# Four steps of a segment-attention loop in another order

## The chip, the cores and the metric

The program runs on one core of a Trainium2 chip. The metric is the device time of one execution in microseconds (us); for the kernel before it is 2229.49 us, the median of three runs (2226.88 to 2230.01).

A core has engines that each work through a queue of their own: TensorE (PE, matrix products, with the weight loads shown apart as PEld), VectorE (DVE), ScalarE (ACT), GpSimd (POOL) and SyncE (SP, which here only issues DMAs). They wait for each other through semaphores. PE writes its results to PSUM, which is divided into banks; the other engines read them there.

## The reference

The network is a decoder of four layers on x of 16 x 256 x 128 floats; each layer has an attention, a cross-attention and a feed-forward part, each followed by a residual and a layer norm. The change lies in one of these twelve parts, the attention of layer L1. Sixteen heads of 8 channels; the 256 positions of a batch form four segments of 64. Each segment attends to itself with all its 64 keys, and to the segments one and two away with every fourth of their keys (SEG is 64, DIL 4, NN 2):

```
def _attn(q, k, v):
    scores = jnp.einsum('bshqd,bshkd->bshqk', q, k) / math.sqrt(q.shape[-1])
    a = jax.nn.softmax(scores, axis=-1)
    return jnp.einsum('bshqk,bshkd->bshqd', a, v)
...
out = _attn(q, k, v)
dil_idx = jnp.arange(0, SEG, DIL)
kd = k[:, :, :, dil_idx, :]
vd = v[:, :, :, dil_idx, :]
seg_ids = jnp.arange(S)
w = 1.0 / (2 * NN)
for off in range(1, NN + 1):
    for sign in (-1, 1):
        n = seg_ids + sign * off
        valid = (n >= 0) & (n < S)
        nc = jnp.clip(n, 0, S - 1)
        cross = _attn(q, kd[:, nc], vd[:, nc])
        out = out + jnp.where(valid[None, :, None, None, None], cross * w, 0.0)
...
return out @ Wo + bo
```

## The kernel before

The whole network is one program; its parts follow one another, with x kept in SBUF in two forms: `xt` (128 positions by 128 channels, 32 tiles) and `xT` (channels by 4096 positions). The part of the change is `layer_a1`. It treats the 16 batches one after another, two batches being a group of 512 positions (8 groups), in a loop over rounds b that is a software pipeline. Products and their users are:

- `project`: one product 128x512 gives q or k of a group in the PSUM bank `m`; ACT adds the bias and writes it to SBUF.
- `keys`: POOL multiplies k of a batch with a mask of heads, once for the own segments (`kb4`) and once for every fourth key (`kbd`). Then a product with 32 rows can treat one head.
- `own_scores` and `far_scores`: scores in two PSUM tiles named `sc`, which ACT turns into exponentials, `eo` and `ed` (the latter is called `e` in the profile).
- `values`: five pairs of small products into `m`; DVE adds the bias and spreads them into `vxs`.
- `sums`: denominators into the bank `den` (products at L340), then numerators of the own segments into `num`; DVE takes the reciprocals (L949) and weights them (L950).
- `scaled`: products that spread the reciprocals over the rows of `ed`, again into the two `sc` tiles, after which DVE multiplies `ed` in place (L969, two instructions); one more product spreads them for the own part, ACT copies it (L971), DVE multiplies (L972).
- `far_sums`: numerators of the far segments; DVE adds both parts to `oTn` (L981).
- `out`: the output product of a group into `m`, then `tail`: DVE adds the residual (L458) and takes statistics (L393, L394), POOL the reciprocal root (L381 to L399). The last step of the norm, on ACT (L404), is put off until `settle` in the next round. `transposed` later turns the finished group back into `xT`: four PE transposes into `m` and a copy on ACT (L355).

Two things set the order. `in_order` ties each PE instruction to the one before it, so that PE works in exactly the order in which the code calls it. On the other engines a planner orders the instructions: GpSimd and VectorE run some of them earlier than the code's order has them (the first two `xb` of L435 stand ahead of the first `keys`, an `oTn` among the statistics of an `out`). The line in force for PSUM is:

```
    with s.banks(sc=(2, 2), den=(1, 1), num=(2, 1), m=(1, 1)), s.in_order(), s.deferring():
```

So there are two `sc` tiles for three users a round (own scores, far scores, the spread reciprocals), and a single bank `m` for `project`, `values`, `transposed` and `out`. All products are issued through the helpers at L336, L340 and L343, so that the profile shows these lines and the tile names tell the steps apart. The DMAs of the part load weights for later parts; no step of the loop issues one.

Of the kernel before, what the change touches and what calls it, by code (L numbers as in the profile page):

```python
# [19 lines left out]
B, S, D, SC = 16, 256, 128, 64  # L20
NT = B * S
NTI = NT // 128
NG = NT // 512
# [629 lines left out]
def evac(s, out, ps, bias=None):  # L653

    if bias is None:
        s.nc.scalar.copy(out, ps)
    else:
        s.nc.scalar.activation(out, ps, AF.Identity, bias=bias)
# [207 lines left out]
def layer_a1(s, w):  # L866
# [16 lines left out]
    q, k, kb, eo, ed, oT, num, rw = {}, {}, {}, {}, {}, {}, {}, {}  # L883

    def project(d, n, g, wt, bias):
        ps = s.bank("m")
        s.mm(ps, wt, s.xT[:, 512 * g:512 * g + 512])
        d[g] = s.work(n, [128, 512])
        evac(s, d[g], ps, bias)

    def keys(b):
        kb[b] = [s.work(n, [128, m, 4, 64]) for n, m in (("kb4", 4), ("kbd", 1))]
        kk = k[b // 2][:, S * (b % 2):S * (b % 2) + S]
        nc.gpsimd.tensor_tensor(kb[b][0], kk.rearrange("p (g k) -> p g k", g=4).unsqueeze(2).broadcast_to([128, 4, 4, 64]),
                                hm4.unsqueeze(1).broadcast_to([128, 4, 4, 64]), ALU.mult)
        nc.gpsimd.tensor_tensor(kb[b][1][:, 0], kk[:, 0:S:4].unsqueeze(1).broadcast_to([128, 4, 64]), hm4, ALU.mult)

    def values(b):
        xb = s.xT[:, S * b:S * b + S]
        ps = s.bank("m")  # L900
        for g in range(5):
            xs = xb[:, 64 * g:64 * g + 64] if g < 4 else xb[:, 0:S:4]
            for a in range(2):
                s.mm(ps[64 * a:64 * a + 64, 64 * g:64 * g + 64], xs, wv[:, :, a, :])
        v = ps[:, 0:320].rearrange("p (g i u d) -> p g i u d", g=5, i=4, u=2)
        dst = vxs[b % 2].rearrange("p g i (u x) -> p g i u x", u=2)
        for a in range(2):
            h = slice(64 * a, 64 * a + 64)
            for u in range(2):
                nc.vector.tensor_tensor(dst[h, :, :, u, 8 * a:8 * a + 8], v[h, :, :, u, :],  # L910
                                        bv[h, :, u, a, :].unsqueeze(1).broadcast_to([64, 5, 4, 8]), ALU.add)

    def own_scores(b):
        qb = q[b // 2][:, S * (b % 2):S * (b % 2) + S]
        sc = [s.bank("sc", [128, 2, 4, 2, 64]) for _ in range(2)]
        for g in range(4):
            for u in range(2):
                for i in range(4):
                    r = slice(32 * i, 32 * i + 32)
                    s.mm(sc[i // 2][:, i % 2, g, u, :], kb[b][0][r, g, 2 * u:2 * u + 2, :].rearrange("p j k -> p (j k)"),  # L920
                         qb[r, 64 * g:64 * g + 64])
        eo[b] = s.work("eo", [128, 4, 4, 2, 64])
        for h in range(2):
            s.latest = nc.scalar.activation(eo[b][:, 2 * h:2 * h + 2], sc[h], AF.Exp, scale=8 ** -0.5)

    def far_scores(b):
        qb = q[b // 2][:, S * (b % 2):S * (b % 2) + S]
        sc = [s.bank("sc", [128, 2, 2, S]) for _ in range(2)]
        for u in range(2):
            for i in range(4):  # L930
                r = slice(32 * i, 32 * i + 32)
                s.mm(sc[i // 2][:, i % 2, u, :], kb[b][1][r, 0, 2 * u:2 * u + 2, :].rearrange("p j k -> p (j k)"), qb[r, :])
        ed[b] = s.work("e", [128, 4, 2, S])
        for h in range(2):
            s.latest = nc.scalar.activation(ed[b][:, 2 * h:2 * h + 2], sc[h], AF.Exp, scale=8 ** -0.5)

    def sums(b):

        den = s.bank("den", [128, 2, S])
        for u in range(2):  # L940
            for i in range(4):
                s.part(den[32 * i:32 * i + 32, 0, :], sd[:, u, :], ed[b][:, i, u, :], u == 0, False)
        for g in range(4):
            for u in range(2):
                for i in range(4):
                    s.part(den[32 * i:32 * i + 32, 0, 64 * g:64 * g + 64], so[:, u, :], eo[b][:, i, g, u, :],
                           False, u == 1)
        rc = s.work("rcT", [128, S])
        nc.vector.reciprocal(rc, den[:, 0, :])  # L949
        nc.vector.tensor_tensor(rc, rc, w["wq"], ALU.mult)  # L950
        rw[b] = den, rc
        num[b] = s.bank("num", [128, 2, S])
        for g in range(4):
            for u in range(2):
                for i in range(4):
                    s.mm(num[b][32 * i:32 * i + 32, 0, 64 * g:64 * g + 64], vxs[b % 2][:, g, i, 32 * u:32 * u + 32],
                         eo[b][:, i, g, u, :], u == 0, u == 1)

    def scaled(b):
        den, rc = rw[b]  # L960
        sc = [s.bank("sc", [128, 2, 2, S]) for _ in range(2)]
        for u in range(2):
            for i in range(4):
                r = slice(32 * i, 32 * i + 32)
                s.mm(sc[i // 2][:, i % 2, u, :], rd[r, u, :], rc[r, :])
        s.mm(den[:, 1, :], w["ro"], rc)
        for h in range(2):
            e = ed[b][:, 2 * h:2 * h + 2]
            nc.vector.tensor_tensor(e, e, sc[h], ALU.mult)  # L969
        ro = s.work("ro", [128, S])  # L970
        nc.scalar.copy(ro, den[:, 1, :])  # L971
        nc.vector.tensor_tensor(ro, ro, num[b][:, 0, :], ALU.mult)  # L972
        rw[b] = ro

    def far_sums(b):
        for u in range(2):
            for i in range(4):
                s.mm(num[b][32 * i:32 * i + 32, 1, :], vxs[b % 2][:, 4, i, 32 * u:32 * u + 32], ed[b][:, i, u, :],
                     u == 0, u == 1)
        oT[b] = s.work("oTn", [128, S], bufs=3)  # L980
        nc.vector.tensor_tensor(oT[b], rw[b], num[b][:, 1, :], ALU.add)  # L981

    def out(g):
        y = s.bank("m", [128, 4, D])
        for j in range(4):
            s.mm(y[:, j, :], oT[2 * g + j // 2][:, 128 * (j % 2):128 * (j % 2) + 128], w["o"])
        s.tail(g, y, s.biased(g, w["r_bo"]), transpose=False, act=True)

    with s.banks(sc=(2, 2), den=(1, 1), num=(2, 1), m=(1, 1)), s.in_order(), s.deferring():
        project(q, "qT", 0, w["q"], w["bq"])  # L990
        project(k, "kTs", 0, w["k"], w["bk"])
        keys(0)
        keys(1)
        values(0)
        project(q, "qT", 1, w["q"], w["bq"])
        own_scores(0)
        far_scores(0)
        for b in range(B + 4):
            if b + 1 < B:
                own_scores(b + 1)  # L1000
            if 1 <= b <= B:
                far_sums(b - 1)
            if b < B:
                sums(b)
            if b + 1 < B:
                far_scores(b + 1)
                values(b + 1)
            s.settle()
            g = (b + 3) // 2
            if g < NG:  # L1010
                project(*((k, "kTs", g, w["k"], w["bk"]) if b % 2 == 0 else (q, "qT", g, w["q"], w["bq"])))
            if b < B:
                scaled(b)
            if b % 2 == 1 and 3 <= b and b // 2 - 2 >= 0 and b // 2 - 2 < NG:
                s.transposed(b // 2 - 2)
            if b % 2 == 1 and 3 <= b <= B + 1:
                out(b // 2 - 1)
            if b + 2 < B:
                keys(b + 2)


def layer_x1(s, w, gate):
# [943 lines left out]
def normalized(s, nd):  # L1966
# [7 lines left out]

LAYERS = (("a0 x0", layer_x0), ("f0", layer_f0),
          ("a1", layer_a1), ("x1", layer_x1), ("f1", layer_f1),
          ("a2", layer_a2), ("x2", layer_x2),
          ("f2 a3", layer_a3), ("x3 f3", layer_last))
# [29 lines left out]
```

## Time and profile before

The profile shows one execution of 2229.6 us, of which the span from the first to the last instruction is 2227.8 us.

| What | Value | How to read it |
|---|---|---|
| PE busy | 1795.3 us, 81% of the span | average over all parts |
| DVE, ACT, POOL busy | 1133.0, 857.9, 811.0 us | 51%, 39%, 36% |
| `layer_a1`, from its first own scores in round 0 to the last transposes | 296.9 to 542.3 us | about a ninth of the span |
| PE busy from 296.9 to 516.3 | 183.95 of 219.40 us | granted clock 0.92 on average there |
| PE busy from 516.3 to 542.3 | 14.60 of 26.00 us | the end of the part, granted clock 0.76 |
| DVE, ACT, POOL busy from 296.9 to 516.3 | 106.95, 84.94, 53.56 us | none is near its limit |

The granted clock is the share of full speed at which PE was allowed to run; in this trace it is 1.0 or 0.5 at any moment, and changes in steps of 3.41 us.

### The profile page before, as it was taken

The numbers are of one execution on the slowest core, as the hardware profiler recorded it, in microseconds if no ns is written. First come the engines' busy times: TensorE is split into PE (matmuls) and PEld (weight loads), VectorE is DVE, ScalarE is ACT, GpSimd is POOL, SyncE is SP. The second block draws the span as 40 slices with busy tenths as digits, with TensorE's granted clock in tenths as the row PEclk, the third lists the DMA queues.
The fourth block names the chain that finished last, engine by engine and source line by source line (L and its number), as shares of the span: only waits on it lengthen the run. The fifth ranks groups of instructions, "written<-read, shape, count | busy, mean of one in ns | idle before, by whom it ended". The sixth has DMA issues, their size and how long they took to land.

```text
span 2227.8 us, 39433 instructions
## 1 busy us (share of the span) xinstructions
PE 1795.3 (81%) x16572; PEld 1132.3 (51%) x16572; DVE 1133.0 (51%) x2808; ACT 857.9 (39%) x1267; POOL 811.0 (36%) x956
## 2 busy tenths in 40 slices
PE   6784388886999836949784789987789988999998
PEld 3451256664777624625452556654445544555554
DVE  5677624544366663145476677746725552322231
ACT  6565633432333201322354222225646653223221
POOL 2432322222244325755434334444536652111110
PEclk8896569997999956969896899988979998999999
DMA  3000000001011221430000000010000000000000
GB/s 114 4 3 21 1 2 3 3 3 45 1 30 29 71 51 45 76 88 0 6 14 20 1 1 1 2 41 23 2 1 2 2 1 1 5 5 5 5 10 10
DMA packets 45649, 41.59 MB, mean 19 GB/s; under 512 B 6880, under 2 KB 42144, under 8 KB 44832
## 3 DMA queue, kind: packets, MB, share of 16 engines
q1 hardware_dynamic: 35456, 31.22, 4.5%
q0 software_dynamic: 5632, 4.33, 1.5%
q10 hardware_dynamic: 4384, 3.52, 0.5%
q8 instruction: 130, 2.13, 0.4%
q14 instruction: 47, 0.39, 0.1%
HBM read 28.44 MB, written 10.62 MB: 18 GB/s over the span
## 4 chain that ended last, share of the span: by engine, by line
PE 56%; DVE 18%; POOL 11%; issue 7%; ACT 5%; DMA 2%; POOLq 0%; DVEq 0%; SPq 0%; ACTq 0%
PE p L336 14%; PE m L336 12%; PE sc L336 11%; PE y L336 6%; PE nd L336 3%; POOL rs L383 2%; PE nd L340 2%; PE den L340 2%; DVE rcT L1969 2%; PE m L343 2%; POOL acc L1318 2%; PE num L336 2%; DVE st L393 1%; ACT xt L404 1%; DVE r L458 1%
## 5 line engine op out<-in xcount | busy, mean ns | idle before, releaser
L336 PE MATMUL p<-h,w_f 128*128 128x512 f32 x512 | 222.3, 592 | 0.4 <-DVE h L1820 0.4
L336 PE MATMUL sc<-qT,kb 32*128 32x256 f32 (+1 forms) x2816 | 184.3, 381 | 42.6 <-DVE qT L650 17.2
L381 POOL TENSOR_SCALAR ve<-mv 128x4 f32<-128x4 f32 x128 | 30.6, 239 | 427.1 <-DVE mv L394 423.7
L336 PEld LDWEIGHTS sc<-qT,kb 32*128 32x128 f32 x2816 | 129.6, 204 | 94.3 <-issue 61.2
L343 PE MATMUL m<-ident,xt 128*128 128x128 f32 x448 | 87.8, 318 | 104.0 <-ACT xt L404 47.4
L336 PEld LDWEIGHTS p<-h,w_f 128*128 128x128 f32 x512 | 96.7, 190 | 119.8 <-issue 117.9
L1905 ACT ACTIVATE e<-sc 128x1024 f32<-128x1024 f32 x128 | 124.0, 1021 | 74.2 <-PE sc L336 73.4
L383 POOL TENSOR_TENSOR rs<-ve,nhalf 128x4 f32<-128x4 f32 x128 | 134.3, 1049 | 6.3
L343 PEld LDWEIGHTS m<-ident,xt 128*128 128x128 f32 x448 | 59.1, 156 | 132.9 <-ACT xt L404 54.8
L393 DVE BATCH_NORM_STATS2 st<-r 128x6 f32<-128x128 f32 x480 | 119.6, 272 | 3.3
L435 POOL TENSOR_TENSOR xb<-xt,r_x 128x512 f32<-128x512 f32 x48 | 60.8, 1271 | 152.2 <-DVE r L1763 76.9
L1969 DVE RECIPROCAL rcT<-nd 128x256 f32<-128x256 f32 x48 | 84.1, 1751 | 62.3 <-PE nd L336 62.3
L355 ACT COPY xT<-m 128x512 f32<-128x512 f32 x104 | 60.0, 581 | 139.2 <-PE m L343 138.5
L404 ACT ACTIVATE xt<-r,nm,rs 128x128 f32<-128x128 f32 x176 | 72.5, 484 | 95.0 <-POOL nm L399 95.0
L1825 ACT ACTIVATE h<-p,w_f 128x512 f32<-128x512 f32 x64 | 44.0, 687 | 153.6 <-PE p L336 153.5
L336 PE MATMUL m<-xT,w_a 128*128 128x512 f32 x144 | 82.0, 685 | 25.7 <-DVE vxs L910 18.9
L407 DVE TENSOR_SCALAR xt<-r,mv,rs 128x128 f32<-128x128 f32 x208 | 66.8, 382 | 59.6 <-POOL rs L383 59.6
L1831 DVE TENSOR_TENSOR ys<-y,r_f 128x512 f32<-128x512 f32 x8 | 5.5, 691 | 175.4 <-PE y L336 175.4
L578 ACT ACTIVATE e<-sc 128x1024 f32<-128x1024 f32 x64 | 61.9, 1019 | 62.6 <-PE sc L336 62.6
L1626 DVE TENSOR_TENSOR a<-sc,cst 128x1024 f32<-128x1024 f32 x64 | 75.0, 1208 | 14.4 <-PE sc L336 14.3
L394 DVE BATCH_NORM_AGGREGATE mv<-st 128x2 f32<-128x6 f32 x512 | 80.7, 167 | 0.1
L1094 ACT ACTIVATE e<-sc 128x1024 f32<-128x1024 f32 x32 | 32.8, 1024 | 110.0 <-PE sc L336 110.0
(423 smaller groups left out, 4075.2 us busy)
## 6 DMA issues: line engine op xcount, KB each, us to landing
acc<-xt SPq DMA_DIRECT2D x16, 256.0 KB, 2.8
mw<-in_moe SPq DMA_DIRECT2D x8, 512.0 KB, 4.1
yx<-acc SPq DMA_DIRECT2D x12, 256.0 KB, 3.6
w_f<-in_w_f SPq DMA_DIRECT2D x1, 2824.0 KB, 10.5
w_x<-in_w_x SPq DMA_DIRECT2D x1, 2336.5 KB, 9.8
xt<-in_x SPq DMA_DIRECT2D x8, 256.0 KB, 7.5
rows<-xn SPq DMA_DIRECT2D x8, 256.0 KB, 2.5
out_x<-xt SPq DMA_DIRECT2D x8, 256.0 KB, 2.3
```

The costliest lines, as they stand in the source:

```text
L336: self.put(self.nc.tensor.matmul(out=out, lhsT=lhsT, rhs=rhs, start=start, stop=stop))
L340: self.put(self.nc.tensor.matmul(out=out, lhsT=lhsT, rhs=rhs, start=start, stop=stop, skip_group_check=True))
L343: self.put(self.nc.tensor.transpose(out, in_, self.ident if ident is None else ident))
L383: nc.gpsimd.tensor_tensor(rs, ve, self.nhalf[:, :n], ALU.pow)
L393: nc.vector.bn_stats(st[:, j, :], r[:, j, :])
L394: nc.vector.bn_aggr(mv[:, j, :], st[:, j, :])
L404: ins, front = nc.scalar.activation(out[:, j, :], r[:, j, :], AF.Identity, bias=nm[:, j:j + 1], scale=rs[:, j:j + 1]), self.latest
L407: ins, front = nc.vector.tensor_scalar(out[:, j, :], r[:, j, :], mv[:, j, 0:1], rs[:, j:j + 1], ALU.subtract, ALU.mult), self.mark
L578: s.latest = nc.scalar.activation(eu, sc[h], AF.Exp, scale=8 ** -0.5)
L1626: s.mark = nc.vector.tensor_tensor(a[:, h, :, :], sc[h].rearrange("p i j k -> p (i j) k"), tri, ALU.mult)
L1905: nc.scalar.activation(e[:, 2 * h:2 * h + 2, :, :], sc[h], AF.Exp, scale=8 ** -0.5)
L1969: s.nc.vector.reciprocal(rc, nd[:, 1, :])
```

## The change

The same instructions are issued, in another order. In a round, the projection moves from behind `values` to ahead of `sums`; the masking of keys moves from the round's end to right behind `sums`; `transposed` moves from odd rounds to the next even round, for which the loop gets one round more. `values` keeps its place behind `far_scores`.

```diff
-        for b in range(B + 4):
+        for b in range(B + 5):
             if b + 1 < B:
                 own_scores(b + 1)
             if 1 <= b <= B:
                 far_sums(b - 1)
+            g = (b + 3) // 2
+            if g < NG:
+                project(*((k, "kTs", g, w["k"], w["bk"]) if b % 2 == 0 else (q, "qT", g, w["q"], w["bq"])))
             if b < B:
                 sums(b)
+            if b + 2 < B:
+                keys(b + 2)
             if b + 1 < B:
                 far_scores(b + 1)
                 values(b + 1)
             s.settle()
-            g = (b + 3) // 2
-            if g < NG:
-                project(*((k, "kTs", g, w["k"], w["bk"]) if b % 2 == 0 else (q, "qT", g, w["q"], w["bq"])))
             if b < B:
                 scaled(b)
-            if b % 2 == 1 and 3 <= b and b // 2 - 2 >= 0 and b // 2 - 2 < NG:
-                s.transposed(b // 2 - 2)
+            if b % 2 == 0 and 0 <= b // 2 - 3 < NG:
+                s.transposed(b // 2 - 3)
             if b % 2 == 1 and 3 <= b <= B + 1:
                 out(b // 2 - 1)
-            if b + 2 < B:
-                keys(b + 2)
```

## The prediction

> **What bounds the stretch.** I read the page first (PE 81% busy, no other engine over 51%), then the chain of waits through the rounds, then the timeline at the end of the loop. The chain has each link's start, length and work:
>
> ```profile
> 362.29 2.00 PE sc L336 x60
> 364.29 1.00 PE num L336 x16
> 365.29 1.76 PE den L340 x80
> 367.04 0.89 PE num L336 x64
> 367.94 1.08 PE sc L336 x16
> 369.01 0.87 PE m L336 x20
> ...
> 371.18 1.10 PE m L336 x2
> 372.28 1.09 PE sc L336 x16
> ...
> 373.39 2.36 DVE e L969 x2
> ...
> 386.88 0.63 PE den L336 x2
> 387.51 0.45 PE m L343 x4
> 387.96 0.02 issue
> 387.98 0.59 ACT xT L355
> 388.58 0.04 issue
> 388.62 1.16 PE m L336 x8
> 389.78 1.94 PE sc L336 x64
> ```
>
> This is round 4, from its own scores at 362.29 through far sums, denominators, numerators, far scores, values, projection and `scaled` to the two DVE multiplications; round 5 starts its own scores at 375.80. So a round is a ring of **13.51 us** in which PE stands still twice: 1.30 us between values (ended 369.88) and projection (371.18), because both use the one bank `m`, which DVE must empty first; and at the end, while DVE multiplies and the `sc` tiles are not free. The last five lines are an odd round with transposes: there the ring doesn't end with DVE but with bank `m` again, transposes, ACT copy, output product.
>
> **Projection ahead of the sums.** In its new place bank `m` was last used by transposes or the output product of the round before. Their readers, the ACT copy (0.59) and the DVE addition (0.69, behind 2.36 of multiplications and 0.41 of L972), are done about 1.1 us after the own scores begin; the projection comes 3.0 us after that. So it doesn't wait, and costs its 1.10 us. Its reader on ACT (0.68) stands behind the own exponentials, which end about 4 us into the round, and is done near 4.8; values want `m` at 7.9. No wait there either.
>
> What is late next, once `scaled` no longer stands behind the projection? Its products need the two `sc` tiles, and those are read by the exponentials of the far scores. Rounds 13 and 14 show it already, since no projection is left for them. Timeline of round 13:
>
> ```profile
> 497.73 1.94 ACT L935 ACTIVATE e<-sc 128x1024 f32<-128x1024 f32 x2 [5.24 <-PE sc L336]
> ...
> 499.72 1.13 PE L336 MATMUL sc<-rcT,w_a 32*128 32x256 f32 x12 [0.21 <-ACT e L935]
> 500.50 2.35 DVE L969 TENSOR_TENSOR e<-e,sc 128x1024 f32<-128x1024 f32 x2 [0.78 <-PE sc L336]
> ```
>
> From the start of the exponentials to that of the multiplications it is 500.50 - 497.73 = 2.77 us (round 14: 513.55 - 510.77 = 2.78). In round 4 it is 373.39 - 369.05 = 4.34. The new round is 2.00 + 1.00 + 1.10 + 1.76 + 0.89 + 1.08 + 0.02 + 2.77 + 2.36 + 0.04 = **13.02 us**, so 0.49 is won, not the 2.4 us of stall and product that leave the old place. The reciprocals are not later: they end 1.76 + 0.42 after the denominators, `scaled` comes 0.89 + 1.08 + 1 after them. Projections exist in rounds 0 to 12: 13 x 0.49 = **6.4 us**. Bounds: 0 if something holds the projection up for half a microsecond, 13 x 1.57 = 20 if it found a gap on PE; there is none in front of the sums, so the lower working stands.
>
> **Keys behind the sums.** Profile of waits: PE waits 7.9 us, in 7 rounds, for POOL's `kb`. But only the first four products of the own scores wait for it (346.52 in round 2, after `kb` of 1.89 us); the other sixty start 0.04 us after the DVE multiplications end (347.16). I cost the removal at 0. The new place gives POOL the masks some 8 us earlier: four instructions, 1.89 + 0.72 twice, 5.2 us in an even round. Queued behind them could be the norm of a group (about 1.8 us on POOL), whose result ACT takes only behind the far exponentials, some 5 us later; that cover suffices. No DMA moves, SP's queue holds nothing of this loop.
>
> **Transposes in even rounds.** In odd rounds 5 to 13 the time from the multiplications' start (386.90) to the end of the own scores (391.72) is 4.82; without transposes the output product starts right behind `den`, 0.63 + 1.16 fit into the 2.36, and it is 2.36 + 0.04 + 2.00 = 4.40. Won: 5 x 0.42 = **2.1 us**. In even rounds 0.63 + 0.45 lie within the 2.36 too: cost 0; without that cover 0.45 each, 8 times.
>
> **The end.** Before, the order in rounds 16 and 17 is transposes of group 6, then the output product of group 7. The chain shows the price:
>
> ```profile
> 531.19 1.65 ACT xt L404 x4
> ...
> 533.40 0.59 ACT xT L355
> ...
> 534.04 2.09 PE m L336 x8
> ```
>
> The output product at 534.04 waits for the norm of group 6, only because of its place. Its own input (`oTn`, L981) is ready at 529.15. After the change group 6 is turned in round 18, and group 5, finished long before, in round 16. The output product can run at 529.2 and, at the full clock that holds until 532.7, end at 530.35 instead of 536.13; the chain behind it (addition, statistics, POOL, norm, last transposes) keeps its 6.2 us. Won: **5.8 us**. The other bound is 0.6: in the code the norm of group 6 (settle of round 16) stands ahead of the ACT copy of group 5's transposes. If ACT keeps that order, bank `m` is free only at 532.85 + 0.59, and the output product starts at 533.5. I take 5.8, since the planner puts `oTn` among the statistics as soon as it is ready, and this is the same case.
>
> **The clock.** A round with half clock is dear: round 1 (own scores 313.61 to 330.39) takes 16.78 us with 6.83 us of half clock, against 13.51, so 0.48 per microsecond. Here a rule speaks against the change, since it takes the projection out of the sparse part of the round. The Trainium skill (page "TensorE: Matmul & The Clock Gate", section "Why this matters for your kernels") says that gaps over some 3 us between bursts bring the half clock back. No gap inside a full round is over 1.6 us, so by the rule neither order loses clock. The windows of 3.41 us (busy: PE, PEld, DVE, ACT, POOL; then the clock) say otherwise:
>
> ```profile
> 344.98:348.39 3.41, 2.03 (x50) 1.53 (x50) 2.46 (x3) 0.37 (x1) 3.41 (x3) 1.00 0.00 0
> 348.39:351.81 3.42, 3.42 (x45) 2.16 (x44) 0.12 (x1) 1.94 (x2) 1.28 (x2) 0.50 0.02 5
> ```
>
> PE was busy for 2.03 of 3.41 us, and the clock halved. A window with 2.09 (355.22) didn't bring it down. When I count each product's columns by the share of the array that it fills (32 of 128 rows: a quarter), the windows (taken 0.2 us earlier) before a half clock have under some 1550 columns, the others more. In the new rounds, the worst window is the end of an even round plus the own scores (1024 columns): under the limit when a window starts within some 0.7 us, one time in five. Rounds 0 to 4, with neither transposes nor, mostly, output products, stay as they were. From 296.9 to 516.3 I count 34 us of half clock before, and about as much after; term 0. Ends: if the early rounds keep their clock, 12 us less, -6; if pairs of rounds lock to the windows (26.0 + 1.5 us is close to 8 windows), one cold window in each of six pairs, 20 us, +10. By the rule the sum is the same, but without these ends.
>
> **Sum.** 6.4 + 2.1 + 5.8 = 14.3 us off the profiled 2229.6: **2215.3**. The profiled execution is the median of the runs to 0.1 us. 1.8 us lie outside the span and stay.
>
> **Rivals.**
> - *ACT keeps the code's order at the end*: 6.4 + 2.1 + 0.6 = 9.1, 2220.5. For it: norm copies of other rounds do follow the code's order. Against: `oTn` and `xb` don't.
> - *Hidden anyway*: the projection in its new place holds up the sums for 0.5 us a round (bank `m`, or ACT behind the exponentials), and the end gives 0.6; 2 to 3 us remain, 2227. Against: 1.9 us of slack at `m`.
> - *The clock decides, slower*: place, the gap between far scores and own scores, which is left with fewer products. If every round loses two windows as rounds 1 and 2 do, that is 16 x 6.8 = 109 us of half clock against 34, + 75 x 0.48 = 36, less 14: 2251. It decides from 34 + 14.3/0.48 = 64 us of half clock on. For it: windows with 2.0 us busy did halve. Against: output products and transposes fill rounds from 5 on.
>
> **How the numbers follow.** A measurement tells apart about 0.2%, 4.5 us. Forecast 0.56; ACT order 0.22; hidden 0.08; clock 0.14. The first two are faster: 0.78; hidden is the same: 0.08; clock: 0.14. The range starts at 2207 (forecast with -6 from the clock and 2 more) and ends at 2225 (forecast plus 10, ACT's order plus 4.5).
>
> **What would show it.** Own scores to own scores about 13.0 us at full clock in rounds 4 to 12, even and odd alike; no wait of the product `m<-xT` for DVE L910, instead one of `sc<-rcT` for ACT L935 in every round; the wait for `kb` gone; the last output product some 5 us behind the last `oTn` no longer, but right behind it. A round over 13.5 at full clock, or over 64 us of half clock before the end of round 14, would make it wrong.

## The result, and the profile after

The changed kernel takes **2213.82 us** (median of four runs, 2209.21 to 2215.31), the kernel before 2228.84 us beside it; the ratio is 0.993, with a 95% interval of 0.9913 to 0.9947. Measured again later it was 2215.64 against 2226.07, ratio 0.9952 (0.9935 to 0.9968). The forecast was 2215.3.

The profiled execution has a span of 2212.7 us, 15.1 less than before. Cut at four events that both traces have, this is where they came from:

| Stretch | Before, us | After, us | Less by |
|---|---|---|---|
| start of the span to the first own exponentials (not touched) | 292.4 | 291.2 | 1.2 |
| **rounds**: to the first of round 15's multiplications (L969) | 231.6 | 226.5 | 5.2 |
| **end**: to the next part's first work on its mask (L1039) | 21.4 | 15.6 | 5.8 |
| rest of the span (not touched) | 1682.4 | 1679.4 | 2.9 |

So 11.0 us lie where the order changed and 4.1 don't; the untouched rest varied from 1679 to 1693 us among the eleven profiles taken later. The two untouched stretches together had 476.9 us of half clock in the profile after, 489.8 before. At the 0.49 us that a microsecond of half clock costs in this part (see the experiments), 12.9 us less are an estimated 6 us, enough for the 4.1. The forecast had 8.5 us for the rounds and 5.8 for the end, 14.3 in all: 3.3 us too much in the rounds. That the total came so close is luck, since the rest of the program made up for it.

The chain of waits, two rounds of the kernel after, from the own scores of round 7 on (start, length, work):

```profile
405.78 2.00 PE sc L336 x60
407.78 1.00 PE num L336 x16
408.79 1.06 PE m L336 x2
409.84 1.89 PE den L340 x80
411.74 0.89 PE num L336 x64
412.63 1.09 PE sc L336 x16
...
414.66 1.03 ACT e L935
415.69 0.04 issue
415.73 0.76 PE sc L336 x8
416.49 0.02 issue
416.51 2.36 DVE e L969 x2
418.87 0.04 issue
418.92 2.00 PE sc L336 x60
420.92 1.00 PE num L336 x16
421.92 1.06 PE m L336 x2
422.97 1.94 PE den L340 x80
...
424.94 1.77 DVE rcT L949
426.71 0.02 issue
426.73 1.77 DVE rcT L950
428.50 0.14 issue
428.63 1.15 PE sc L336 x10
```

The first round is the forecast ring: the projection (408.79) stands ahead of the denominators, and ScalarE's exponentials, not bank `m`, hold up `scaled`. It takes 13.14 us. The next, an even round, is closed by something else: VectorE's product L950, which took 0.42 us before, now takes 1.77, and `scaled` waits for it. That round takes 13.29 (418.92 to 432.21).

The end of the loop, again from the chain:

```profile
520.40 1.07 PE num L336 x16
521.47 0.60 PE m L343 x4
522.07 0.02 issue
522.09 0.59 ACT xT L355
522.69 0.04 issue
522.73 1.17 PE m L336 x8
```

Far sums, the transposes of group 5 with their copy, and at once the last output product. The norm of group 6, for which the output product stood still before, is no longer in this chain. The copy (522.09) comes ahead of that norm on ACT, which the timeline has at 524.40.

### The profile page after: what moved, and what is told of

Read it like the earlier page. It is cut to its first block, busy times and chain, and to the rows that moved or that the text cites. A ratio compares the mean times of both kernels' runs of the same rounds, so it can differ in the third digit from the quotient of the medians.

```text
span 2212.7 us, 39445 instructions
## 1 busy us (share of the span) xinstructions
PE 1801.2 (81%) x16571; PEld 1135.5 (51%) x16572; DVE 1140.7 (52%) x2808; ACT 858.7 (39%) x1267; POOL 811.7 (37%) x956
## 4 chain that ended last, share of the span: by engine, by line
PE 56%; DVE 19%; POOL 11%; issue 7%; ACT 5%; DMA 1%; POOLq 0%; DVEq 0%; SPq 0%; ACTq 0%
PE p L336 15%; PE m L336 11%; PE sc L336 11%; PE y L336 6%; PE nd L336 3%; POOL rs L383 2%; PE nd L340 2%; PE den L340 2%; DVE rcT L1969 2%; PE m L343 2%; DVE e L969 2%; POOL acc L1318 2%; DVE st L393 1%; PE num L336 1%; DVE r L458 1%
## 5 line engine op out<-in xcount | busy, mean ns | idle before, releaser
L381 POOL TENSOR_SCALAR ve<-mv 128x4 f32<-128x4 f32 x128 | 30.7, 240 | 420.0 <-DVE mv L394 416.6
L1905 ACT ACTIVATE e<-sc 128x1024 f32<-128x1024 f32 x128 | 124.1, 1021 | 74.1 <-PE sc L336 73.3
L578 ACT ACTIVATE e<-sc 128x1024 f32<-128x1024 f32 x64 | 61.9, 1019 | 61.4 <-PE sc L336 61.4
L435 POOL TENSOR_TENSOR xb<-xt,r_a 128x512 f32<-128x512 f32 x24 | 30.7, 1283 | 131.8 <-DVE r L458 130.6
```

The costliest lines, as they stand in the source:

```text
L435: self.nc.gpsimd.tensor_tensor(t, self.xt[:, 4 * g:4 * g + 4, :], row.unsqueeze(1).broadcast_to([128, 4, D]), ALU.add)
L1905: nc.scalar.activation(e[:, 2 * h:2 * h + 2, :, :], sc[h], AF.Exp, scale=8 ** -0.5)
```

## The experiments

The experiments ran in three groups, each on one chip together with the kernel before, whose own median was 2235.47, 2224.26 and 2226.07 us in the three. Since these medians move by more than most effects here, the table gives the stretches of the profile too, each from one execution; "half clock" is the time at clock 0.5 within the rounds. "Product in the gap" is explained below.

| Kernel | Median, us | Ratio to before (95%) | Rounds, us | Half clock, us | End, us |
|---|---|---|---|---|---|
| before | | | 231.6 | 42.3 | 21.4 |
| after | 2213.82 | 0.993 (0.9913 to 0.9947) | 226.5 | 45.4 | 15.6 |
| after, second time | 2215.64 | 0.9952 (0.9935 to 0.9968) | 225.7 | 44.8 | 15.7 |
| projection alone | 2240.13 | 1.0019 (1.0005 to 1.0033) | 234.9 | 56.1 | 21.3 |
| projection and keys | 2238.93 | 1.001 (0.9995 to 1.0025) | 235.1 | 56.1 | 21.3 |
| transposes alone | 2224.06 | 0.9946 (0.9932 to 0.9961) | 229.5 | 42.8 | 15.7 |
| end alone | 2233.72 | 0.9981 (0.9964 to 0.9997) | 233.8 | 45.2 | 15.1 |
| after, reciprocals in PSUM | 2209.35 | 0.9924 (0.9895 to 0.9952) | 218.5 | 32.4 | 15.6 |
| after + product in the gap | 2199.38 | 0.9878 (0.9849 to 0.9908) | 210.0 | 11.8 | 15.4 |
| both | 2200.07 | 0.988 (0.9849 to 0.9911) | 209.2 | 11.7 | 15.4 |
| before + product in the gap | 2214.81 | 0.9944 (0.9921 to 0.9967) | 216.7 | 14.5 | 21.2 |
| projection alone + product | 2213.75 | 0.9948 (0.9929 to 0.9967) | 215.0 | 12.0 | 21.3 |
| transposes alone + product | 2209.73 | 0.9924 (0.9904 to 0.9944) | 216.0 | 15.6 | 15.5 |

**One part of the change at a time.** The projection alone:

```diff
+            g = (b + 3) // 2
+            if g < NG:
+                project(...)
             if b < B:
                 sums(b)
...
-            g = (b + 3) // 2
-            if g < NG:
-                project(...)
```

> Only the projection moves ahead of the sums; keys and transposes stay where they were. Ring theory: the round at full clock falls from 13.5 to 13.0 us in rounds 0 to 12, 6.4 us in all, before what the clock adds or takes (0.48 us for each us of half clock more or less); the total is 2222 to 2225. The product behind the far scores then waits for ScalarE's exponentials and no longer for bank m. Rival (the early key masks bring the gain): without them less than 2 us are won, and the own scores wait for the masks as before.

It is slower than before, by 0.2% and just clear of noise. The stall at bank `m` did go (2.77 instead of 4.34 us from the exponentials to the multiplications in odd rounds), but half clock rose by 13.8 us. The windows of 3.41 us (busy: PE, PEld, DVE, ACT, POOL; then the clock) show how:

```profile
398.92:402.34 3.42, 2.27 (x30) 1.40 (x28) 3.15 (x5) 1.64 (x5) 0.01 (x1) 1.00 0.00 0
402.34:405.75 3.41, 3.41 (x64) 3.22 (x64) 0.01 (x1) 0.50 (x1) 0.00 (x0) 0.50 0.02 5
...
429.64:433.06 3.42, 2.26 (x39) 1.40 (x31) 2.88 (x4) 1.37 (x4) 0.00 (x0) 1.00 0.02 5
433.06:436.47 3.41, 3.41 (x60) 2.89 (x56) 0.00 (x0) 1.02 (x2) 0.00 (x0) 0.50 0.00 0
```

The half clock returns after 30.72 us, nine windows: two rounds, lengthened by the half clock itself, take 30.4 us, close to nine windows, and so the end of each of these even rounds meets a window boundary in nearly the same bad place. The prediction had such a lock, with eight windows, as the upper end of its range.

With the keys as well:

```diff
                 sums(b)
+            if b + 2 < B:
+                keys(b + 2)
...
-            if b + 2 < B:
-                keys(b + 2)
```

> Projection and keys move, transposes stay. Ring theory: as with the projection alone, within 2 us, because the wait for the masks was hidden behind VectorE's multiplications. Lock theory (found in the profile after): with keys early, the masks on GpSimd run beside VectorE's product L950, which then takes up to 1.9 us instead of 0.42 in even rounds; that costs 0.2 us a round, under 2 us in all, so this is equal or up to 2 us slower than the projection alone. Rival (masks bring the gain): clearly faster than the projection alone.

Nothing tells it from the projection alone: rounds of 235.1 against 234.9, and from round 2 on L950 takes 1.76 to 1.89 us in even rounds of both. In both, the first mask waits for ACT to write k (`kTs`): what brings the masks forward is the arrival of k, not the place of `keys` in the code.

The transposes alone:

```diff
-            if b % 2 == 1 and 3 <= b and b // 2 - 2 >= 0 and b // 2 - 2 < NG:
-                s.transposed(b // 2 - 2)
+            if b % 2 == 0 and 0 <= b // 2 - 3 < NG:
+                s.transposed(b // 2 - 3)
```

> Only the transposes move to even rounds; projection and keys stay. Ring theory: 2.1 us from five odd rounds and 5.8 us at the end, 7.9 us: 2221, plus or minus what the clock makes of it. Rival (the end was worth nothing by itself, as the chain there is set by the norm): 2 us at most, 2227.

Rounds 2.2 us shorter, the end 5.7 us. This is the larger part of what the change brought. (The profile is of its slowest run, 2230.23 us; the median is 12 us below before, more than these stretches explain.) And the end alone, with the order of before up to round 16:

```diff
+            if b == B + 1:
+                out(b // 2 - 1)
             if b % 2 == 1 and 3 <= b and ...:
                 s.transposed(b // 2 - 2)
-            if b % 2 == 1 and 3 <= b <= B + 1:
+            if b % 2 == 1 and 3 <= b < B + 1:
                 out(b // 2 - 1)
```

> The order of before, save that in round 17 the last output product goes ahead of the transposes of group 6. Ring theory: from the start of the last multiplications to the end of the last transposes 18.2 us become about 12.4 to 13, 5 to 5.8 us less, total 2223. Rival (the norm sets that end): no change.

The end fell from 21.4 to 15.1 us; the total by 0.19% (0.03 to 0.36), less than the 5 to 5.8 us expected, in which 2.2 us more in the rounds are contained, with 2.9 us more half clock.

**The product L950.** In the kernel after, the timeline of round 4 shows GpSimd's masks and VectorE's product side by side (start, length, engine):

```profile
370.25 1.90 POOL L894 TENSOR_TENSOR kb<-kTs,cst 128x1024 f32<-128x1024 f32 x1
370.60 1.82 DVE L950 TENSOR_TENSOR rcT<-rcT,w_a 128x256 f32<-128x256 f32 x1
```

In the same round of the kernel before, the masks came only after the product:

```profile
368.90 0.42 DVE L950 TENSOR_TENSOR rcT<-rcT,w_a 128x256 f32<-128x256 f32 x1
...
373.16 1.89 POOL L894 TENSOR_TENSOR kb<-kTs,cst 128x1024 f32<-128x1024 f32 x1 [6.75 <-ACT kTs L658]
```

Both of L950's operands lie in SBUF. In the kernel after it ends at 372.42, 0.27 us after the mask has ended at 372.15: it looks as if it stood still until about the end of the mask. The test leaves the reciprocals in PSUM, so that only one operand comes from SBUF:

```diff
-        nc.vector.reciprocal(rc, den[:, 0, :])
-        nc.vector.tensor_tensor(rc, rc, w["wq"], ALU.mult)
+        nc.vector.reciprocal(den[:, 0, :], den[:, 0, :])
+        nc.vector.tensor_tensor(rc, den[:, 0, :], w["wq"], ALU.mult)
```

> The kernel after, with the reciprocals written back to PSUM, so that L950 reads one operand from SBUF and one from PSUM. Lock theory: L950 takes about 0.42 us in every round, also beside the masks on GpSimd (it was 1.8 in even rounds), and the multiplications of even rounds start 2.77 instead of 2.99 us behind the exponentials: 7 x 0.2 = 1.5 us less than after, if the clock is the same. Rival (ScalarE's exponentials set that point in every round): L950 gets short but the round stays as it is.

```profile
366.96 1.90 POOL L894 TENSOR_TENSOR kb<-kTs,cst 128x1024 f32<-128x1024 f32 x1
...
367.32 0.42 DVE L950 TENSOR_TENSOR rcT<-den,w_a 128x256 f32<-128x256 f32 x1
```

Beside the same mask it now takes 0.42 us, and every full-clock round from 4 to 12 takes 13.13 us, even and odd alike. This agrees with the mechanism that the Trainium skill states (page "SBUF — State Buffer", section "SBUF: two separate sides"): VectorE with two SBUF inputs and a GpSimd instruction that reads SBUF take a shared pair of ports in turn, for a whole instruction. The rounds fell by 8 us, but 13 us less half clock come with that, so most of it isn't the product's; beside the additional product of the next test, where the clock is out of play, it is worth 0.8 us (210.0 to 209.2), and the total shows no difference.

**The clock.** An additional product in the gap ahead of the own scores, its result read by nobody:

```diff
+    def filler(n):
+        s.mm(s.bank("m")[:, 0:n], w["q"], s.xT[:, 0:n])
...
                 scaled(b)
+            if b + 2 < B and (b % 2 == 0 or b == 1):
+                filler(256 if b >= 6 else 512)
```

> The kernel after, with an additional product whose result nobody reads in the gap in front of the own scores, in even rounds and in round 1 (512 columns, 256 from round 6 on). Clock theory (a window of 3.41 us whose products fill the array too little is followed by half clock): half clock between the first own scores and the end of round 14 falls from 41 us to under 15, and the total falls by 0.48 x 26 = 12 us, to about 2202. Rival (only gaps over 3 us count, none is here): half clock stays, and the total stays or rises by up to 0.3 us a round.

The rounds of the kernel after without and with it (columns as above; the granted clock is the 0.90 and the 0.97):

```profile
291.20:517.66 226.46, 203.08 (x4441) 144.82 (x4441) 116.81 (x206) 88.63 (x121) 54.59 (x58) 0.90 0.02 5
...
292.20:502.20 210.00, 192.98 (x4458) 139.07 (x4457) 117.80 (x206) 88.61 (x121) 54.67 (x58) 0.97 0.02 5
```

Half clock in the rounds fell from 45.4 to 11.8 us, all that is left being before round 1, and the rounds by 16.5 us: 0.49 us for each microsecond. More work made the kernel faster. With both edits:

> Both: the product in the gap and the reciprocals in PSUM. If both theories hold, the gains add: about 2200.5. It is the candidate for a version that beats both kernels.

2200.07 us, the same as without the reciprocals' edit within what can be told. The product in the kernel before:

> The kernel before, with the additional product (512 columns) in the gap of even rounds and of round 1. Clock theory: its 34 us of half clock between the first own scores and the end of round 14 fall to under 15, and the total by 9 us or more, to about 2219, so that most of the distance between before and after could be had without the change of order. Rival: no change.

14.9 us less in the rounds, more than the whole reordering won there, and 0.9944 in all.

What a window must hold to keep the clock can be counted. Take each product's columns times the share of the 128 x 128 array that it fills, and add them up over a window of 3.41 us. In the thirteen profiles, from 292 to 545 us, windows with under 1510 such columns were followed by half clock and the others by full clock, with 5 exceptions among 965; within each profile alone, some limit between 1490 and 1590 has none. TensorE's busy time, with the best limit for each profile, misplaces 133. Over the whole executions (bf16 columns counted at a quarter) 1510 misplaces 5 to 10 of some 645 windows in each profile, mostly between 182 and 204 us, in another part. This is a count and not a test: no run filled the gap with narrow products.

**The two moves without the clock.** The projection alone and the transposes alone, each with the product in the gap:

> The projection alone ahead of the sums, with the additional product (512 columns) in even rounds and round 1. If the projection alone lost only because its even rounds end in a gap that brings half clock, its stretch from the first own exponentials to the last multiplications (234.9 us with 56 us of half clock) falls to about 213 us, about 4 us under the kernel before with the same additional product (216.7), and the whole is faster than the kernel before by about 16 us. Rival (the projection costs PE time in its new place, whatever the clock): the stretch stays above 217.

> The transposes alone in even rounds, with the additional product (256 columns from round 6 on). Without half clock, what is left is the wait of the output product for bank m in odd rounds: the stretch is about 216.7 - 2.1 = 214.6 us, and the end is 15.5 instead of 21.3 us. If both moves add up when the clock is out of play, the projection alone, this one and the kernel after with the same product stand at about 213, 214.6 and 210. Rival (the transposes help only through the clock): 216.7 in the stretch.

The time of two full-clock rounds, an odd and an even one, from rounds 7 and 8 of the four profiles. The product there has 512 columns where the transposes are in odd rounds and 256 otherwise; that doesn't matter, since the kernels before and after without it, also at full clock there, take the same two sums to 0.01 us:

| | transposes in odd rounds | transposes in even rounds |
|---|---|---|
| projection behind the values | 14.09 + 13.33 = 27.42 | 13.51 + 13.51 = 27.02 |
| projection ahead of the sums | 14.10 + 13.12 = 27.22 | 13.13 + 13.30 = 26.43 |

Alone, the moves win 0.20 and 0.40, together 0.99. I expected stretches of 214.6 us for the transposes with the product and 213 for the projection; they were 216.0 and 215.0. The transposes' profile still has one window of half clock in round 10, which takes 15.19 instead of 13.51 us; that accounts for the difference. For the projection, the chain of waits in one of its odd rounds has the reason:

```profile
376.94 1.13 PE sc L336 x12
378.07 0.63 PE den L336 x2
378.70 0.45 PE m L343 x4
379.15 0.02 issue
379.17 0.59 ACT xT L355
379.77 0.04 issue
379.81 1.16 PE m L336 x8
```

With transposes in the odd round, the ring doesn't end with VectorE (which starts at 377.72, when 8 of the 12 are done) but with PE's own order: all of `scaled`, transposes, copy, output product, 380.97. From the exponentials to the end of `scaled` are 3.13 us, 1.21 less than 4.34, and the projection in its new place costs about that. The move pays in an odd round only if the transposes leave it.

The kernel after once more:

> The kernel after as it is, on this chip. Its stretch is 226.5 us with 45 us of half clock in the profile so far. Its even rounds have a gap that halves the clock at some positions of the 3.41 us windows only, so half clock in the stretch may be 30 to 50 us and the stretch 218 to 228; the ratio to before stays near 0.993.

Half clock 44.8 us again, but in other rounds: now also in 7 and 9, no longer in 1.

## Why the prediction came out as it did

- **The ring** (13.51 to 13.02): right in kind, 0.11 to 0.27 too short. One term mis-sized is the cost of the projection in its new place, put at its own 1.10: from the own scores to the end of the denominators the chain grew from 4.75 (362.29 to 367.04) to 5.96 us (405.78 to 411.74), so by 1.21. The denominators are not slower (about 1.95 us from the first one's start to the last one's end in both kernels, by the timeline); before, they began 0.19 us before the far sums ended, which is why the chain gave them only 1.76. That is 13 x 0.11 = 1.4 us. Even rounds lose 0.16 more through L950, 1.1 us in seven rounds. I had looked at GpSimd's queue for what the early masks would delay, and not at what runs on VectorE at the same time; "the reciprocals are not later" was the wrong sentence.
- **What is won without the clock**: 8.5 predicted for the rounds. The two kernels with the product in the gap differ by 6.7, of which 2.7 us less half clock make 1.3; 5.4 remain. The 1.4 and 1.1 account for most of the missing 3.1.
- **The parts as a sum**: the step "13 x 0.49 = 6.4" took the projection's gain as independent of where the transposes are. It isn't: in odd rounds it exists only together with the other move. The sum of both was still right, since I worked the odd round of the changed kernel out as a whole.
- **Keys at 0**: right for the move of `keys`, which changed nothing beside the projection. The wait for `kb` fell from 12.2 us on PE's weight loads to one of 1.5, but the projection alone brings the masks as early, so what the lost wait is worth was not tested by itself.
- **Transposes 2.1**: 2.2 measured. **The end 5.8**: 5.8 measured; the planner did put the copy of group 5 first, so the rival "ACT order" fell.
- **The clock at 0**: 3.1 us more half clock in the profile, about 1.5 us lost. The lock of two rounds to the windows, which I had as the range's upper end, is what made the projection alone slower: with the product in the gap, it is 1.7 us faster than before in the rounds (215.0 against 216.7). With the transposes in the even rounds' gap the half clock was 11 us less, and no lock followed; this I read off the profiles, no run tests it alone. Term 0 was thus near the measured value partly by luck.
- **The rule of the Trainium skill** ("TensorE: Matmul & The Clock Gate", "Why this matters for your kernels"), gaps over some 3 us: the longest in rounds 1 to 13 of the kernel before was 1.33 us, and yet removing the sparse windows gave 16.5 us. Here the measurement decides. The prediction's count by filled columns stands, with a limit near 1510 instead of 1550.

What stays open: why the parts outside had 12.9 us less half clock, though the instructions there have the same order, save near the part itself; and the rest of the 3.1 us.

## What to carry to other kernels

Work the round out as a ring with every engine's next event in it, for odd and even rounds together: a stall that goes uncovers the next one (here 2.4 us left the old place and 0.4 were won a round), and two moves can each be worth little and together much. Before moving work out of a sparse stretch of TensorE, look at the granted clock by windows of 3.41 us: here the filling of the gap was worth more than the removal of the wait. And when an operation of GpSimd moves, see which of VectorE's products with two SBUF operands it will now run beside.

The kernel after with the product in the gap beats both kernels: 0.9878 of before (0.9849 to 0.9908), where the change alone has 0.993 and 0.9952 (measured in other groups).

## What the hardware showed that was not expected

- By the count over 965 windows, the clock goes with the share of the array that is filled (5 misplaced) and not with the time that TensorE is busy (133): a window with 2.27 us of matmuls and 1463 filled columns was followed by half clock (398.92, projection alone), one with 2.09 us and 1765 columns wasn't (355.22, before). A product of 0.6 to 1.1 us in every second round, for nobody, took 34 us of half clock away.
- Two rounds can lock to the clock's windows (27.4 us against the 27.3 of 8 windows before, 30.4 against 30.7 of 9 with the projection alone), so that the same code met half clock in each pair of rounds from 6 to 11, or in none for 109 us.
- VectorE's product with two SBUF operands took 1.77 to 1.89 us instead of 0.42 beside a GpSimd mask; with one operand in PSUM it stayed at 0.42 beside the same mask.
